# A two-layer graph network: layer 0 with paired logits, moments taken once per step, layer 1's preparation inside step 2, repair by a branch, and masks on ScalarE

## The chip, the cores and the metric

The kernel runs on one core of a Trainium2 chip. The metric is the device time of one execution, in microseconds (us). A core has five engines with queues of their own: PE (TensorE, matrix products; PEld are its weight loads), DVE (VectorE), ACT (ScalarE), POOL (GpSimd) and SP (SyncE, which here issues transfers). Operands lie in SBUF, results of matrix products in PSUM. "Profile" and "trace" below mean one execution recorded by the hardware profiler; its times are from the start of that execution's span.

## The reference, cut to what matters

A graph of N = 3327 nodes with D = 256 features passes through two layers. Each layer normalises its input, applies a relu, runs a graph network and adds the result to its input.

```python
def top_p_attention(X):                       # A: (N, N), rows sum to 1
    q = X @ W1.T @ W2.T                       # 64 wide
    k = X @ W3.T
    probs = softmax(q @ k.T)
    sp = sorted(probs, descending)            # per row
    keep = cumsum(sp) - sp < 0.9
    A = probs * mask(keep)
    return A / A.sum(-1)

# layer 0
h = relu(layernorm(x))
R = adj + I;  R = R / R.sum(-1)
Xf = Xa = h;  Z = 0
for n in range(2):
    A  = top_p_attention(Xa)
    Xf = R @ Xf                               # "full step"
    Xa = A @ Xa                               # "attention step"
    Z  = Z + Xf @ U1[n].T + Xa @ U2[n].T      # "add up"
x = x + layernorm(h + Z) * g + b

# layer 1, 4 heads of 64
h = relu(layernorm(x));  hp = h @ W
s, d = hp . a_src, hp . a_dst                 # per node and head
e = where(adj > 0, leaky_relu(s_i + d_j), -inf)
x = x + elu(softmax(e) @ hp)
```

## The kernel before

The nodes are cut into 26 row tiles of 128 (the last has 127 rows). Everything that is used often stays in SBUF: `main` holds h (with a column of ones, so that a product with it gives row sums as well), `xf1` and `xa1` the two results of step 0. A tile framework puts the instructions of all engines into an order by its own list scheduling, so the order on an engine's queue is not that of the program's text.

**Beginning (L542-557).** All 26 tiles of x are loaded and their moments taken; then one Sqrt for all; then each tile is normalised and passed through a relu.

**Keys (L797-810), once per step.** For each tile: two transposes (L563), the projection by W3 to keys as columns (L571, copied into `kt` at L802), the same as rows (L805), and a product that sums up the keys' second moments and means (L809).

**Pairs of tiles (L811-832).** Row tiles go in 13 pairs. `exponentials` (L574-610) projects the two tiles' queries (L571, L587), multiplies them with the moments (L591), from which DVE gets the mean and variance of each row's logits, and then computes the logits, per tile seven pieces of 512 columns with a depth of 64 (L604), each followed by an exponential on ACT that also sums (L605). The exponentials of the next pair are called before the pair in hand is cut.

**`top_p` (L612-730)** finds for each row the value below which the entries sum to a tenth of the row. A start value comes from the mean and variance by a polynomial, with four ACT calls, Ln and Exp in turn (L630, L631, L633, L645, L648). Then `below` (L655-665) passes over the 3327 entries of each of the two tiles, 3 times in step 0 and 4 times in step 1 (`EVALS`), with some 17 operations on two columns between passes (L672-691). A last pass (L705) writes the entries below a safe bound; from 16 pieces of 208 columns the eight largest are taken (L703), from those the 32 largest (L713, L715), and their running sum tells the cut. L730 zeroes what lies below the cut. How many of the 32 places are used, and some other values, are left in `met`.

**`full_step` (L734-746)** multiplies a tile's column block of the adjacency (two loads of 13 blocks, L739, on SP's queue) with h or xf1: 26 products of 128 rows, each of which the trace records as two instructions (so L741 has 52 per tile), divides by the row sums and writes the next Xf. **`attention_step` (L748-770)** transposes the 26 blocks of a tile's cut exponentials in groups of four (L757, copied at L759) and multiplies them with Xa (L766). In step 1, **`add_up` (L772-793)** loads x once more for h, transposes the four results and multiplies them with U1 and U2.

**Layer 1's preparation (L842-905)** follows when all tiles are done: layernorm, sum with x, a second layernorm and relu, transposes, one product with W and the two attention vectors (L895), and the scaling of hp (L898).

**Layer 1 (L907-999)** takes blocks of four row tiles (the last block two), and for every two column tiles j: a load of adjacency (L939), one mask of up to 1024 columns on POOL (L943), eight products of exponentials with the mask on DVE (L953), eight products with hp into the two halves of two accumulators (L963) and eight of `den` (L968), again two instructions each in the trace. Then each tile is transposed, divided, passed through elu and written (L978-999).

**Verdict (L1004-1034).** From `met` and the reach of s and d comes one flag, `redo`. If it is set, a slower general form computes everything again behind a branch (L1041).

Of the kernel before, what the change touches and what calls it, by code (L numbers as in the profile page):

```python
# [18 lines left out]
P = 128  # L19
N = 3327  # L20
NT = 26
# [20 lines left out]
EVALS = (3, 4)  # L42
AIM = 13.0
WIN = 32
PIECES = 16
PIECE = 208
NC = 7

REACH = 40.0
QUANTILE = (0.0080475, 0.1178442, 0.6505088, 2.0535298, 1.2031906)  # L50
# [416 lines left out]

@with_exitstack
def fast(
    ctx: ExitStack,  # L470
    tc: tile.TileContext,
    redo: bass.AP,
# [15 lines left out]
    V, S, T = nc.vector, nc.scalar, nc.tensor  # L488

    const = ctx.enter_context(tc.tile_pool(name="const", bufs=1))  # L490
    ident = const.tile([P, P], F32, name="ident")
    make_identity(nc, ident)
    eps = const.tile([P, 1], F32, name="eps")
    nc.gpsimd.memset(eps, LN_EPS)
# [3 lines left out]
    mv = const.tile([P, NT, 2], F32, name="mv")  # L498
    rstd = const.tile([P, NT], F32, name="rstd")

    met = const.tile([P, 5, STEPS * NT], F32, name="met")

    def ln_stats(pool, t):
        st = pool.tile([P, V.BN_STATS_DIM], F32, name="bst")
        V.bn_stats(st, main[:, t, :D])
        V.bn_aggr(mv[:, t, :], st)

    def ln_rstd():
        S.activation(rstd, mv[:, :, 1], AF.Sqrt, bias=eps)
        V.reciprocal(rstd, rstd)  # L510

    def ln_apply(dst, src, mean, rs):
        V.tensor_scalar(dst, src, mean, rs, ALU.subtract, ALU.mult)

    with ExitStack() as l0:
        wpool = l0.enter_context(tc.tile_pool(name="wpool", bufs=1))
        w1 = wpool.tile([P, 2, DA], F32, name="w1")
        w3 = wpool.tile([P, 2, DA], F32, name="w3")
        w2 = wpool.tile([DA, DA], F32, name="w2")
        u1 = wpool.tile([P, STEPS, 2, D], F32, name="u1")  # L520
        u2 = wpool.tile([P, STEPS, 2, D], F32, name="u2")
        h_mv = wpool.tile([P, NT, 2], F32, name="h_mv")
        h_rstd = wpool.tile([P, NT], F32, name="h_rstd")
        xf1 = wpool.tile([P, NT, D + 1], F32, name="xf1")
        xa1 = wpool.tile([P, NT, D + 1], F32, name="xa1")
        kt = wpool.tile([DA, NP], F32, name="kt")
        gm = wpool.tile([DA, 2 * DA + 1], F32, name="gm")
        V.tensor_copy(gm[:, :DA], ident[:DA, :DA])

# [3 lines left out]
        apool = l0.enter_context(tc.tile_pool(name="apool", bufs=2))  # L533
        etpool = l0.enter_context(tc.tile_pool(name="etpool", bufs=2))
        fin = l0.enter_context(tc.tile_pool(name="fin", bufs=1))
        ps_l = l0.enter_context(tc.tile_pool(name="ps_l", bufs=2, space=PSUM))
        ps_acc = l0.enter_context(tc.tile_pool(name="ps_acc", bufs=2, space=PSUM))
        ps_t = l0.enter_context(tc.tile_pool(name="ps_t", bufs=2, space=PSUM))
        ps_m = l0.enter_context(tc.tile_pool(name="ps_m", bufs=2, space=PSUM))


        for t in range(NT):  # L542
            nc.sync.dma_start(main[:, t, :D], x[t * P : (t + 1) * P, :])
            ln_stats(small, t)
        nc.scalar.dma_start(w1, w1t.rearrange("(c p) o -> p c o", p=P))
        nc.scalar.dma_start(w3, w3t.rearrange("(c p) o -> p c o", p=P))
        nc.scalar.dma_start(w2, w2t)
        nc.scalar.dma_start(u1, u1t.rearrange("n (c p) o -> p n c o", p=P))
        nc.scalar.dma_start(u2, u2t.rearrange("n (c p) o -> p n c o", p=P))
        ln_rstd()  # L550
        V.tensor_copy(h_mv, mv)
        V.tensor_copy(h_rstd, rstd)
        for t in range(NT):
            ln_apply(main[:, t, :D], main[:, t, :D], mv[:, t, 0:1], rstd[:, t : t + 1])
            S.activation(main[:, t, :D], main[:, t, :D], AF.Relu)
        for z in (main, xf1, xa1):
            nc.gpsimd.memset(z[:, :, D : D + 1], 1.0)

        def transposed(src, t):

            ps = ps_m.tile([P, 2, P], F32, name="pm")
            for c in range(2):
                T.transpose(ps[:, c, :], src[:, t, c * P : (c + 1) * P], ident)  # L563
            xt = small.tile([P, 2, P], F32, name="xt")
            S.copy(xt, ps)
            return xt

        def projected(w, xt):
            ps = ps_m.tile([DA, P], F32, name="pm")
            for c in range(2):  # L570
                T.matmul(ps, w[:, c, :], xt[:, c, :], start=(c == 0), stop=(c == 1))  # L571
            return ps

        def exponentials(src, tiles):  # L574


            G = len(tiles)
            sm = small.tile([P, G], F32, name="sm")
            mu = small.tile([P, G], F32, name="mu")
            sq = small.tile([P, G], F32, name="sq")  # L580
            es = []
            for g, t in enumerate(tiles):
                ps = projected(w1, transposed(src, t))
                ut = small.tile([DA, P], F32, name="ut")
                S.copy(ut, ps)
                ps = ps_m.tile([DA, P], F32, name="pm")
                T.matmul(ps, w2, ut, start=True, stop=True)  # L587
                qt = small.tile([DA, P], F32, name="qt")
                S.copy(qt, ps)
                ps = ps_m.tile([P, 2 * DA + 1], F32, name="pm")  # L590
                T.matmul(ps, qt, gm, start=True, stop=True)  # L591
                qg = small.tile([P, 2 * DA + 1], F32, name="qg")
                S.copy(qg, ps)
                V.tensor_copy(mu[:, g : g + 1], qg[:, 2 * DA :])
                V.scalar_tensor_tensor(
                    qg[:, :DA], qg[:, :DA], 1.0, qg[:, DA : 2 * DA], ALU.mult, ALU.mult, accum_out=sq[:, g : g + 1]
                )
                e = epool.tile([P, NP], F32, name="e")
                nc.gpsimd.memset(e[:, N:], 0.0)  # L599
                parts = small.tile([P, NC], F32, name="parts")  # L600
                for c in range(NC):
                    w = min(512, N - 512 * c)
                    pl = ps_l.tile([P, 512], F32, name="pl")
                    T.matmul(pl[:, :w], qt, kt[:, 512 * c : 512 * c + w], start=True, stop=True)  # L604
                    S.activation(  # L605
                        e[:, 512 * c : 512 * c + w], pl[:, :w], AF.Exp, accum_out=parts[:, c : c + 1]
                    )
                V.tensor_reduce(sm[:, g : g + 1], parts, AX.X, ALU.add)
                es.append(e)
            return es, sm, mu, sq  # L610

        def top_p(es, sm, mu, sq, n, tiles):  # L612
# [4 lines left out]
            G, i0 = len(es), n * NT + tiles[0]  # L617

            def small_tile(name):
                return small.tile([P, G], F32, name=name)  # L620

            b = small_tile("b")
            V.tensor_scalar(b, sm, 1.0 - TOP_P, None, ALU.mult)
            V.tensor_copy(met[:, 0, i0 : i0 + G], sm)
            var = small_tile("var")
            V.tensor_mul(var, mu, mu)
            V.tensor_sub(var, sq, var)
            V.tensor_scalar(var, var, 1e-6, None, ALU.max)
            sg = small_tile("sg")
            S.activation(sg, var, AF.Ln)  # L630
            S.activation(sg, sg, AF.Exp, scale=0.5)  # L631
            u = small_tile("u")
            S.activation(u, b, AF.Ln, scale=1.0 / N)  # L633
            V.tensor_sub(u, u, mu)
            V.scalar_tensor_tensor(u, var, -0.5, u, ALU.mult, ALU.add)
            V.tensor_scalar(u, u, -6.0, -0.3, ALU.max, ALU.min)
            w = small_tile("w")
            V.tensor_scalar(w, u, QUANTILE[0], None, ALU.mult)
            for c in QUANTILE[1:-1]:
                V.scalar_tensor_tensor(w, w, c, u, ALU.add, ALU.mult)  # L640
            V.scalar_tensor_tensor(w, w, QUANTILE[-1], sg, ALU.add, ALU.add)
            t = small_tile("t0")
            V.tensor_mul(t, w, sg)
            V.tensor_add(t, t, mu)
            S.activation(t, t, AF.Exp)  # L645
            g = small_tile("g0")
            V.tensor_mul(g, w, w)
            S.activation(g, g, AF.Exp, scale=0.5)  # L648
            V.scalar_tensor_tensor(g, g, math.sqrt(2 * math.pi) / N, sg, ALU.mult, ALU.mult)
            V.tensor_scalar(g, g, 0.25, None, ALU.min)  # L650

            k2 = small_tile("k2")
            V.scalar_tensor_tensor(k2, t, 225.0, t, ALU.mult, ALU.mult)

            def below(th, outs=None, dst=None):  # L655
                sums = small_tile("sums") if dst is None else dst
                ys = []
                for k, e in enumerate(es):
# [4 lines left out]
                    if outs is not None:  # L663
                        outs(k, y)
# [130 lines left out]
        for n in range(STEPS):  # L795
# [17 lines left out]
            for i, tiles in enumerate(groups):  # L813
                es, sm, mu, sq = ready
                if i + 1 < len(groups):
                    ready = exponentials(srca, groups[i + 1])
# [264 lines left out]
```

## Time and profile before

| | us |
|---|---|
| median of 3 runs (3064.71 to 3064.73) | 3064.73 |
| profiled execution | 3067.3 |
| its span | 3065.5 |
| mean granted PE clock | 0.919 |

| stage of the profiled execution | from, us | to, us |
|---|---|---|
| loads, layernorm and relu | 0 | 24 |
| keys of step 0 | 24 | 110 |
| first exponentials and first cut of step 0 | 110 | 221 |
| pairs of step 0 | 221 | 1129 |
| keys of step 1 | 1129 | 1200 |
| first cut of step 1 | 1200 | 1312 |
| pairs of step 1 | 1312 | 2355 |
| layer 1's preparation | 2355 | 2453 |
| layer 1 | 2453 | 3056 |

Busy time over the whole span: PE 2730.0 (89%), PEld 1727.1, DVE 2379.9 (78%), ACT 832.9 (27%), POOL 384.6 (13%). A share of busy time is a mean over stages with different limits, so the stages are read one by one. In the views below, "x728" is a count, "out<-in" are the program's names and shapes, and "idle before, releaser" is the time in which the engine stood still before a group of instructions, with the instruction that ended most of it. PEclk is the share of full speed that the throttle granted to TensorE. The 26 loads of 128 KB of x took 2.0 to 3.4 us from issue to landing, the adjacency loads of 832 KB 4.5 us.

### The profile page before, as it was taken

The numbers are of one execution on the slowest core, as the hardware profiler recorded it, in microseconds if no ns is written. First come the engines' busy times: TensorE is split into PE (matmuls) and PEld (weight loads), VectorE is DVE, ScalarE is ACT, GpSimd is POOL, SyncE is SP. The second block draws the span as 40 slices with busy tenths as digits, with TensorE's granted clock in tenths as the row PEclk, the third lists the DMA queues.
The fourth block names the chain that finished last, engine by engine and source line by source line (L and its number), as shares of the span: only waits on it lengthen the run. The fifth ranks groups of instructions, "written<-read, shape, count | busy, mean of one in ns | idle before, by whom it ended". The sixth has DMA issues, their size and how long they took to land. (4 is left out here: it accounts for less than half of the span.)

```text
span 3065.5 us, 35025 instructions
## 1 busy us (share of the span) xinstructions
PE 2730.0 (89%) x12508; PEld 1727.1 (56%) x12508; DVE 2379.9 (78%) x5887; ACT 832.9 (27%) x2029; POOL 384.6 (13%) x258
## 2 busy tenths in 40 slices
PE   6949999999999999389999999999996499999997
PEld 4427676666666685157776666666775322222232
DVE  3189888878788820899988888888983798999996
ACT  2423333333333324232333333333221300000000
POOL 0000000000000000000000000000001157656543
PEclk9759899999999999589999999999998799999999
DMA  3001111111111111001111111110111132232221
GB/s 109 23 0 45 45 45 45 45 45 45 45 45 45 45 56 34 0 4 49 49 49 47 48 47 49 37 37 27 49 60 41 32 118 76 72 94 87 85 62 29
DMA packets 77224, 150.87 MB, mean 49 GB/s; under 512 B 5489, under 2 KB 63600, under 8 KB 77040
## 3 DMA queue, kind: packets, MB, share of 16 engines
q1 hardware_dynamic: 74656, 146.56, 15.3%
q8 instruction: 100, 1.64, 0.2%
q10 hardware_dynamic: 2384, 1.98, 0.2%
q14 instruction: 84, 0.69, 0.1%
HBM read 145.11 MB, written 3.41 MB: 48 GB/s over the span
## 5 line engine op out<-in xcount | busy, mean ns | idle before, releaser
L953 DVE SCALAR_TENSOR_TENSOR e<-both,low,mask 128x512 f32<-128x512 f32 (+1 forms) x728 | 518.0, 781 | 21.0 <-POOL mask L943 15.2
L660 DVE SCALAR_TENSOR_TENSOR y<-e,nt 128x3327 f32<-128x3327 f32 x130 | 478.8, 3683 | 2.3
L604 PE MATMUL pl<-kt,qt 64*128 64x512 f32 (+1 forms) x728 | 408.8, 701 | 53.4 <-ACT e L605 53.4
L759 ACT COPY et<-pt 128x512 f32<-128x512 f32 (+1 forms) x364 | 199.4, 555 | 739.1 <-PE pt L757 739.1
L963 PE MATMUL acc<-e,hp 128*64 128x512 f32 (+1 forms) x1456 | 366.0, 578 | 3.2 <-DVE e L953 3.1
L943 POOL TENSOR_SCALAR mask<-adjb 128x1024 bf16<-128x1024 f32 (+1 forms) x91 | 322.0, 3546 | 240.1 <-DVE e L953 168.3
L741 PE MATMUL acc<-main,at 128*128 128x257 f32 x1352 | 335.1, 400 | 0.8 <-DMA at<-in_adjt_dram 0.8
L741 PE MATMUL acc<-xf,at 128*128 128x257 f32 x1352 | 334.1, 396 | 0.3 <-ACT xa L770 0.3
L766 PE MATMUL acc<-xa,et 128*128 128x257 f32 x1352 | 322.5, 382 | 3.8 <-ACT et L759 3.8
L766 PE MATMUL acc<-main,et 128*128 128x257 f32 x1352 | 323.2, 382 | 0.2
L604 PEld LDWEIGHTS pl<-kt,qt 64*128 64x128 f32 x728 | 144.8, 223 | 291.7 <-ACT e L605 228.4
L741 PEld LDWEIGHTS acc<-main,at 128*128 128x128 f32 x1352 | 261.2, 199 | 52.6 <-issue 13.3
L757 PE MATMUL pt<-ident,e 128*128 128x128 f32 x1352 | 202.1, 274 | 94.0 <-DVE e L730 94.0
L741 PEld LDWEIGHTS acc<-xf,at 128*128 128x128 f32 x1352 | 255.3, 197 | 48.8 <-issue 14.0
L766 PEld LDWEIGHTS acc<-xa,et 128*128 128x128 f32 x1352 | 245.2, 191 | 36.8 <-ACT et L759 7.6
L766 PEld LDWEIGHTS acc<-main,et 128*128 128x128 f32 x1352 | 244.9, 190 | 35.5 <-ACT et L759 6.2
L599 POOL MEMSET e<- 128x1 f32 x52 | 4.9, 98 | 2013.5 <-PE pt L757 1090.1
L605 ACT ACTIVATE e<-pl 128x512 f32<-128x512 f32 (+1 forms) x364 | 205.1, 564 | 154.4 <-PE pl L604 151.4
L757 PEld LDWEIGHTS pt<-ident,e 128*128 128x128 f32 x1352 | 168.6, 141 | 127.7 <-DVE e L730 95.2
L703 DVE MAX8 cands<-y 128x8 f32<-128x208 f32 x832 | 237.2, 360 | 0.5
L963 PEld LDWEIGHTS acc<-e,hp 128*64 128x64 f32 x1456 | 104.1, 136 | 226.3 <-DVE e L953 125.5
L968 PE MATMUL den<-e,qd 128*32 128x512 f32 (+1 forms) x1456 | 200.9, 582 | 0.0
(186 smaller groups left out, 2656.3 us busy)
## 6 DMA issues: line engine op xcount, KB each, us to landing
at<-in_adjt_dram SPq DMA_DIRECT2D x104, 832.0 KB, 4.5
adjb<-in_adjt_dram SPq DMA_DIRECT2D x78, 512.0 KB, 3.8
main<-in_x_dram SPq DMA_DIRECT2D x26, 128.0 KB, 3.4
xh<-in_x_dram SPq DMA_DIRECT2D x26, 128.0 KB, 2.0
xr<-in_x_dram SPq DMA_DIRECT2D x26, 128.0 KB, 2.1
adjb<-in_adjt_dram SPq DMA_DIRECT2D x13, 256.0 KB, 2.8
out_dram<-r SPq DMA_DIRECT2D x25, 128.0 KB, 1.7
u<-in_u1t_dram ACTq DMA_DIRECT2D x1, 512.0 KB, 5.8
```

What stands on the lines that cost most here:

```text
L604: T.matmul(pl[:, :w], qt, kt[:, 512 * c : 512 * c + w], start=True, stop=True)
L605: S.activation(e[:, 512 * c : 512 * c + w], pl[:, :w], AF.Exp, accum_out=parts[:, c : c + 1])
L660: V.scalar_tensor_tensor(y, e[:, :N], th[:, k : k + 1], e[:, :N], ALU.is_lt, ALU.mult, accum_out=sums[:, k : k + 1])
L703: V.max(cands[:, k, c, :], y[:, c * PIECE : min(c * PIECE + PIECE, N)])
L741: T.matmul(acc, at[:, j - j0, :], src[:, j, :], start=(j == 0), stop=(j == NT - 1))
L757: T.transpose(pt[:, k, :], e[:, (j0 + k) * P : (j0 + k + 1) * P], ident)
L759: S.copy(et[:, :n, :], pt[:, :n, :])
L766: T.matmul(acc, et[:, j - j0, :], src[:, j, :], start=(j == 0), stop=(j == NT - 1))
L943: nc.gpsimd.tensor_scalar(mask[:, :, :n, :], adjb[:, :n].rearrange("p i j q -> p j i q"), 0.0, None, ALU.is_gt)
L953: V.scalar_tensor_tensor(e[:, k, :w], both[:, k, :w], low[:, j, k : k + 1], mask[:, j - j0].rearrange("p i q -> p (i q)")[:, :w], ALU.max, ...
L963: T.matmul(acc[k // 2][half, :w], hp[:, j, k, :], e[:, k, :w], start=(j == 0), stop=(j == NT - 1))
L968: T.matmul(den[32 * k : 32 * k + 32, :w], qd[:, j, k : k + 1].to_broadcast([P, 32]), e[:, k, :w], start=(j == 0), stop=(j == NT - 1), tile ...
```

## The change

The numbers of lines are those of the changed kernel from here on.

**Beginning.** Each tile is normalised on its own: moments on DVE, the inverse root as a power on GpSimd (`normal`, L507-516), normalisation and relu as one ACT call.

**Keys and queries together (L614-665).** W1 and W2 are multiplied once into one matrix, and `wqk` holds it beside W3, so that one product (L626) gives a tile's queries in one half of the 128 rows and its keys in the other; even and odd tiles have the halves in turn. The keys are also copied to the other half by a transfer from SBUF to SBUF (L629), on SP's queue. So `kt` holds all keys twice, and `qq` the queries of an even tile in rows 0 to 63 and those of the odd one in rows 64 to 127. Mean and variance of the logits of all rows are computed once per step, behind the keys (L649-665), instead of per pair.

```diff
-                    T.matmul(pl[:, :w], qt, kt[:, 512 * c : 512 * c + w], start=True, stop=True)
+                for g in range(2):
+                    half = slice(g * DA, g * DA + DA)
+                    T.matmul(pl[:, g, :w], qq[half, i, :], kt[half, lo : lo + w], start=True, stop=True)
```

**`top_p` (L685-812).** The start value is worked out on GpSimd, with a power in place of the logarithms, and two Exp forms on ACT:

```diff
-EVALS = (3, 4)
+EVALS = (2, 4)
...
-            S.activation(sg, var, AF.Ln)
-            S.activation(sg, sg, AF.Exp, scale=0.5)
...
-            S.activation(u, b, AF.Ln, scale=1.0 / N)
...
+            GP.tensor_mul(v, b, cn[:, both])
+            GP.tensor_scalar(v, v, math.exp(-6.0), math.exp(-0.3), ALU.max, ALU.min)
+            GP.tensor_tensor(v, v, powers[:, 2, :2], ALU.pow)
+            GP.tensor_scalar(w, v, QUANTILE[0], QUANTILE[1], ALU.mult, ALU.add)
+            GP.tensor_mul(w, w, v)
+            GP.tensor_scalar(w, w, QUANTILE[2], None, ALU.add)
+            GP.tensor_mul(w, w, v)
+            GP.tensor_add(w, w, zadd[:, both])
```

Step 0 has one pass of `below` fewer. The passes write what nobody reads as BF16. The last pass (L776) goes over each tile in two halves, and the eight largest are taken from 13 pieces of 256. The final mask (L808) also sums what it keeps, so that the attention step needs no column of ones.

**`full_step` (L816-836)** loads pieces of 7 blocks into three buffers (before, 13 into two), and has an accumulator of its own beside that of the attention. The row sums are kept from step 0 for step 1. The transposes, the projections and `add_up` share one PSUM pool of two buffers, `ps_x`. In the program's text the attention of a pair now stands ahead of its full steps.

**`add_up` (L861-907)** takes in all of layer 1's preparation: x is loaded, the two layernorms and the sum are done for one tile, the new x is written to DRAM (`x1s`, L888, SP's queue), the transposes and the product with W follow at once (L895, L900), and `main` takes hp in place of h. The weights of layer 1 are prepared at the beginning (`layer1_weights`, L595).

**Repair.** After each step, `amend` (L964-993) works out a flag for each row tile and one over all, and branches on it; behind the branch stands, for each tile, another branch around `search_again` (L909-962), which computes the tile's logits again, finds the cut bit by bit and repeats the tile's attention (in step 1 its full step and `add_up` too):

```diff
+            with tc.If(nc.values_load(flags[:, NT:], min_val=0, max_val=1) > 0):
+                for t in range(NT):
+                    with tc.If(nc.values_load(flags[:, t : t + 1], min_val=0, max_val=1) > 0):
+                        search_again(n, t)
...
+            for bit in range(BITS - 1, -1, -1):
+                V.tensor_scalar(cand.bitcast(I32), cut.bitcast(I32), 1 << bit, None, ALU.bitwise_or)
+                y = scr.tile([P, N], BF16, name="y")
+                V.scalar_tensor_tensor(y, e[:, :N], cand, e[:, :N], ALU.is_ge, ALU.mult, accum_out=sums)
+                V.tensor_tensor(ok, sums, th, ALU.is_ge)
+                V.copy_predicated(cut, ok, cand)
```

The flag at the end, `again`, depends on the reach of s and d alone, and the general form stands behind it as before.

**Layer 1 (L1023-1120).** The masks move to ACT, in two passes, and x is read back from DRAM at the end of a tile:

```diff
+                S.activation(adjb[:, :n], adjb[:, :n], AF.Relu)
                 mask = mpool.tile([P, JC, K, P], BF16, name="mask")
-                nc.gpsimd.tensor_scalar(
-                    mask[:, :, :n, :], adjb[:, :n].rearrange("p i j q -> p j i q"), 0.0, None, ALU.is_gt
-                )
+                S.activation(mask[:, :, :n, :], adjb[:, :n].rearrange("p i j q -> p j i q"), AF.Sign)
...
+                x1 = opool.tile([P, D], F32, name="x1", bufs=4)
+                nc.sync.dma_start(x1, x1s[t])
```

## The prediction

> **What bounds the kernel now.** First the busy time by stretches: the keys of step 0, its start, one pair of row tiles in step 0 and one in step 1, layer 1's preparation, one block of four tiles in layer 1.
>
> ```profile
> core 0: us, PE busy (x) PEld busy (x) DVE busy (x) ACT busy (x) POOL busy (x), PEclk, DMA share, GB/s
> 24.00:110.00 86.00, 77.66 (x430) 53.24 (x430) 10.22 (x35) 33.03 (x112) 2.55 (x26) 1.00 0.12 41
> 110.00:222.00 112.00, 65.92 (x124) 28.41 (x124) 67.39 (x205) 39.64 (x102) 0.00 (x0) 0.50 0.00 0
> 578.00:656.00 78.00, 74.69 (x319) 54.48 (x318) 61.31 (x168) 26.37 (x63) 0.20 (x2) 0.93 0.16 50
> ...
> 1730.00:1818.00 88.00, 83.13 (x370) 61.82 (x369) 75.43 (x198) 29.06 (x67) 0.20 (x2) 0.96 0.15 48
> 2355.00:2455.00 100.00, 38.76 (x174) 29.13 (x175) 72.02 (x220) 26.05 (x85) 25.25 (x28) 0.69 0.16 49
> 2650.00:2740.00 90.00, 86.92 (x445) 24.39 (x443) 84.81 (x123) 5.40 (x10) 59.93 (x17) 0.98 0.28 81
> ```
>
> PE (second figure) fills the pairs, DVE is close behind; at the start and in the preparation neither is full. Layer 1 has PE and DVE both near full. Then the groups, for who waits for whom:
>
> ```profile
> L953 DVE SCALAR_TENSOR_TENSOR e<-both,low,mask 128x512 f32<-128x512 f32 (+1 forms) x728 | 518.0, 781 | 21.0 <-POOL mask L943 15.2
> L660 DVE SCALAR_TENSOR_TENSOR y<-e,nt 128x3327 f32<-128x3327 f32 x130 | 478.8, 3683 | 2.3
> L604 PE MATMUL pl<-kt,qt 64*128 64x512 f32 (+1 forms) x728 | 408.8, 701 | 53.4 <-ACT e L605 53.4
> ...
> L757 PE MATMUL pt<-ident,e 128*128 128x128 f32 x1352 | 202.1, 274 | 94.0 <-DVE e L730 94.0
> ```
>
> The last figure of L757 is the start of each step: PE idle 94.0 in two waits for the first mask. L604's 53.4 is PE waiting for the exponentials. Last the timeline of one layer 1 block:
>
> ```profile
> 2619.37 21.09 DVE L953 SCALAR_TENSOR_TENSOR e<-both,low,mask 128x512 f32<-128x512 f32 x27
> ...
> 2626.34 3.15 POOL L943 TENSOR_SCALAR mask<-adjb 128x1024 bf16<-128x1024 f32 x1 [2.94 <-DVE e L953]
> ...
> 2632.43 3.14 POOL L943 TENSOR_SCALAR mask<-adjb 128x1024 bf16<-128x1024 f32 x1 [2.94 <-DVE e L953]
> ```
>
> One mask, so eight e (two j, four heads), every 6.09 us. An e lasts 740 ns at least, and one beside each mask 1520. So the stages end at 110 (keys 0), 221 (first attention), 1129 (step 0), about 1200 and 1312 (the same in step 1), 2355, 2453 and 3056; the span is 3065.5, the profiled time 3067.3. The median shown, 3064.7, is 2.6 less, which I take off at the end.
>
> **The change, part by part.**
>
> **Start to first attention, 221 to 170.** The barrier over all 26 moments goes, so PE starts near 8 instead of 24. Keys take 26 x 1.5 (eight small matmuls at .15 to .3) = 39; 3.7 full steps that the emitted order puts among them 46 (52 matmuls at .237 = 12.35 per tile); seven paired logits 6.4: end at 100. Each tile's keys also go to the other 64 rows by a DMA on SP's queue, between the adjacency loads (nearest rows: x's 128 KB, 2.0 to 3.4 us); the next tile's work covers it, and without that cover it would cost up to 3.4 once, at the last tile. New moments: four matmuls, products and 52 narrow matmuls, 8; their chain of nine small operations at .195 with one exponential 3. GpSimd's start value follows: ten links, between .1 (its 128x1 memset, 98 ns) and .84 (its 128x256 neg) each, no small arithmetic being in this trace; I take .3, nearer the memset in size: 3, ends 1 to 8.4. It replaces four ACT calls whose table loads alone took 4 x 1.28. ACT's exponential of the start value (L711) waits for this chain, and behind it in ACT's queue stand copies of transposes (L850) for which PE waits. top_p of step 0: four passes at 3.61 (L660 start to start) 14.4; two rounds of small operations 27 x .195 = 5.3, and a few before and behind 1; window 7.3; 26 MAX8 at .33 (.276 for 208, scaled) 8.6; two tiles' wins 5.2; two masks 7.2: 49. In DVE's emitted order two passes of the next pair stand ahead of the mask: 7.2. Sum 8 + 39 + 46 + 6.4 + 11 + 3 + 49 + 7.2 = 169.6. Gain 51.
>
> **Step 0, 908 to 772.** Rows 0-63 and 64-127 work side by side in the paired logits. L604 takes .454 per 512 columns; in L963, whose column halves lie side by side already, one takes .224 to .264, about half. So a pair's logits go from 12.7 + 2.4 stall to 6.4, and are then held by 14 exponentials at .60 on ACT: 8.4. One query and three small projections per tile go from inside the pairs to the keys. A pair then is full steps 24.7 + attention 29.5 (as timed in one pair) + 8.4 + 1.4 fill = 64 on PE, while DVE needs 49 + 5 = 54 (one secant pass per tile fewer). Six full steps (74) are emitted before the first attention and owed no longer, so the first four pairs run at DVE's 54. 4 x 54 + 7 x 64 + 54 + 53.5 for the end = 772. If the halves didn't run side by side, a pair is 70.
>
> **The branch after a step, 10 each.** Twelve small DVE operations 2.3, a matmul, and loads of a flag into every engine that branches; the end of the kernel shows one such load and branch as 3065.5 - 3056.4 = 9.1 together with its shutdown. Ends 4 and 20. Nothing hides it: all queues stand at it.
>
> **Keys of step 1 to first attention, 182 as 80 + 11 + 3 + 70 + 7 = 171.** 80 as in step 0, less x; top_p has two more rounds (2 x (7.2 + 3.3)).
>
> **Step 1, 1043 to 1097.** DVE: 28.9 for passes, 7.3 window, 8.6, 5.2, 7.2, 14 of small operations, and layer 1's preparation, which comes in here: two tiles x 3 (moments .41 + .17 twice, and four 128x256 operations at .42): 77. PE: 24.7 + 29.5 + 8.4 + two add-ups at 5.5 + 2 x 1.4 (L890 and L895) = 76.5. Before: 88 by PE 83 and DVE 75. But the loop is not free: logits of pair i+2 wait for buffers of pair i, then the start value, two passes, the mask of pair i+1, its attention and add-up, which share two PSUM buffers (ps_x) with the transposes. Against a floor of 78 and 10 for each link that DVE's order puts in front (two passes 7.2, start value 3), I take 86; ends 78 and 96. 12 x 86 + 65 for the last = 1097. The x1 rows written to DRAM stand on SP's queue ahead of adjacency loads (832 KB, 4.5 us to land); three buffers of 7 blocks instead of two of 13 cover 21 matmuls, 5.0 us, so a write that waits for DVE longer than that shows up as a PE wait for at.
>
> **Preparation, 98 to 8.** It leaves only layer 1's broadcasts and first mask. Its cover is the pair above; if DVE binds there, its 6 per pair return.
>
> **Layer 1, 603 to 539.** Masks go to ACT: two passes of 1024 at .832 ns per element (512 and 256 copies .585, .372) = 2.1 per pair of j, in an engine busy 5.4 of 90. Then DVE is 8 x .665 = 5.33, and PE 3.58 + 1.85 = 5.43 (acc with DVE ahead, den): 5.45 instead of 6.08. 91 x .63 = 57; less the 7 of its own start, 539. Masks on ACT may bring table loads at 1.28 beside 8 exponentials per block: 20 of 71, hidden. x1 read back: 26 loads of 128 KB, 2.0 each, hidden behind den.
>
> The Trainium skill's page "ScalarE: Activation LUTs" (Rules for kernel authors) wants relu and the like on VectorE. By the row of a 256-wide DVE TENSOR_SCALAR, .305 start to start, a 1024 mask is at most 1.2 there, which makes DVE 5.33 + 1.2 = 6.5 per pair of j, more than now; ACT is the better place here.
>
> **Sum.** 170 + 772 + 10 + 171 + 1097 + 10 + 8 + 539 + 9 = 2786; less 2.6, 2783.
>
> **The rivals.**
>
> *GpSimd is blocked by DVE's passes.* For: the e beside each POOL mask doubled, 740 to 1520 ns, so the two engines do stop each other. Against: that mask is 1024 wide, the new operations two. If each of ten links waits half a pass, 1.8, the chain is 21 instead of 3. In the pairs of both steps half of that is outside the cover of DVE's other work: 24 x 6 + 2 x 18 = 180. 2963; with a third of it 2845.
>
> The Trainium skill's page "SBUF — State Buffer" (Who interferes with whom) says a DVE instruction with two SBUF inputs contends with a GpSimd instruction that reads SBUF, the other then blocking for the whole of it. It speaks against this start value; taken at a full pass per link it makes the chain 36 and the time some 3100. The trace shows the doubling for e alone.
>
> *The halves of the paired logits run one after the other.* L963's row speaks against. 26 x 4.3 less what DVE hides in step 1: 2783 + 90 = 2873.
>
> *The loop of step 1 is covered, and PE binds at 78 a pair.* 12 x 8 = 96 less, 10 in step 0: 2677. For: DVE had 61 of 78 busy with the same passes while PE ran free.
>
> *Slower: repair is taken.* A tile whose search fails costs 27 passes at 3.61 + .8 = 119, eight more passes 29, logits, copies and exponentials 12, attention 15: 175, and nothing overlaps it, since it stands in a branch. The gain is 282; two failing tiles and it is gone: 3133. One row of 3327 is enough for a tile. For: step 0 has one secant pass fewer and a cheaper start value. Against: before, too, a failing row sent the kernel through the general form, and its time shows none; the search, worked through in single precision on the reference's inputs, leaves 1 to 23 of its 32 places used, so some rows are near the lower end.
>
> **How the numbers follow.** My sum .60, own range 2720 to 2850; blocked GpSimd .15; halves in turn .07; covered loop .10; repair or anything slower .06 (.01 of it near no change); two or three small losses together fill the last .02, at 2850 to 2930. The time is that of the first, 2783. Ends that matter: 12 x 8 or 10 in step 1, 57 in layer 1 if nothing is won there, 2 x 10 at the branches. 2660 leaves out about .04 below, 2940 about .14 above (most of the first rival, and the last). What a measurement here can tell from no change is 0.2%, some 6 us. Faster .93, same .01, slower .06.
>
> **What would show it.** The first attention near 170; one pair in steady step 0 at 64 with ACT, not PE, behind the logits; step 1 at 86 with PE waiting for the mask of L808; no DVE stretch of e above 750 ns and 5.45 per pair of j; each branch some 10 of empty queues. A chain of GpSimd operations longer than 5, with gaps the length of a pass, is the first rival; instructions of search_again in the trace (27 passes in a row) are the last. It is wrong above all if step 1's pairs lie outside 78 to 96, since that counts twelvefold.

## The result, and the profile after

The changed kernel takes 3278.2 us in the median of 4 runs (3272.5 to 3281.7) against 3064.7 before: the ratio is 1.069, interval 1.067 to 1.071. The forecast was 2783. It is the last rival that came: two row tiles of step 1 go through the repair.

This is the changed kernel by stretches of the profiled execution (span 3279.8 us): keys of step 0, its first cut, one pair of step 0, one of step 1, the repair, one block of layer 1. The columns are those of the first table in the prediction.

```profile
core 0: us, PE busy (x) PEld busy (x) DVE busy (x) ACT busy (x) POOL busy (x), PEclk, DMA share, GB/s
24.00:134.00 110.00, 96.59 (x490) 62.19 (x488) 29.00 (x156) 36.63 (x101) 18.57 (x64) 0.92 0.23 66
134.00:218.00 84.00, 67.42 (x243) 44.84 (x241) 56.82 (x144) 13.05 (x47) 20.38 (x30) 0.79 0.20 58
600.00:666.00 66.00, 59.98 (x288) 46.77 (x287) 48.81 (x122) 17.96 (x49) 6.64 (x16) 0.99 0.19 56
1820.00:1901.00 81.00, 72.94 (x350) 57.76 (x346) 73.65 (x184) 21.97 (x56) 15.16 (x26) 0.96 0.17 49
2225.00:2697.00 472.00, 100.65 (x348) 70.32 (x348) 294.80 (x331) 28.75 (x47) 5.23 (x12) 0.57 0.04 11
2790.00:2873.00 83.00, 82.33 (x432) 22.12 (x426) 71.75 (x117) 31.66 (x39) 4.76 (x4) 1.00 0.33 95
```

A pair of step 0 went from 78 to 66, one of step 1 from 88 to 81, a block of layer 1 from about 89 to 83. The fifth line is new: 472 us in which PE is busy for a fifth. The groups of the page say what runs there:

```profile
L848 PE MATMUL px<-ident,e 128*128 128x128 f32 x1404 | 218.2, 282 | 359.8 <-DVE e L948 269.9
...
L936 DVE SCALAR_TENSOR_TENSOR y<-e,cand 128x3327 bf16<-128x3327 f32 x54 | 199.0, 3686 | 1.8
```

L936 is a pass of the bitwise search in `search_again`, 27 to a tile; x54 are two tiles. L848, the transposes of the repaired tile's exponentials, idles 269.9 for L948, the last operation of that search that writes them, in two waits. The count of L848 says the same: 1404 = 54 x 26, where 52 tiles and steps need 1352.

### The profile page after: what moved, and what is told of

Same layout as the page of the kernel before. It is cut to its first block, busy times and chain, and to the rows that moved or that the text cites. A ratio compares the mean times of both kernels' runs of the same rounds, so it can differ in the third digit from the quotient of the medians.

```text
span 3279.8 us, 35848 instructions
## 1 busy us (share of the span) xinstructions
PE 2580.6 (79%) x12414; PEld 1697.5 (52%) x12414; DVE 2420.4 (74%) x5386; ACT 818.1 (25%) x1853; POOL 377.9 (12%) x706
## 3 DMA queue, kind: packets, MB, share of 16 engines
q10 hardware_dynamic: 2656, 2.05, 0.2%
## 5 line engine op out<-in xcount | busy, mean ns | idle before, releaser
L848 PE MATMUL px<-ident,e 128*128 128x128 f32 x1404 | 218.2, 282 | 359.8 <-DVE e L948 269.9
L850 ACT COPY et<-px 128x512 f32<-128x512 f32 (+1 forms) x378 | 204.5, 556 | 822.6 <-PE px L848 822.2
L848 PEld LDWEIGHTS px<-ident,e 128*128 128x128 f32 x1404 | 180.1, 146 | 404.2 <-issue 288.0
L729 DVE SCALAR_TENSOR_TENSOR y<-e,nt 128x3327 bf16<-128x3327 f32 x104 | 383.0, 3683 | 1.8
L826 PE MATMUL accf<-xf,at 128*128 128x256 f32 x1456 | 363.4, 396 | 5.3 <-DVE xf L835 5.2
L857 PE MATMUL acca<-main,et 128*128 128x256 f32 x1352 | 334.3, 393 | 40.4 <-ACT et L850 40.3
L857 PE MATMUL acca<-xa,et 128*128 128x256 f32 x1456 | 356.5, 391 | 10.7 <-ACT et L850 10.7
L826 PE MATMUL accf<-main,at 128*128 128x257 f32 x1352 | 330.9, 396 | 23.7 <-issue 18.9
L1078 PE MATMUL acc<-e,main 128*64 128x512 f32 (+1 forms) x1456 | 347.3, 577 | 0.7 <-DVE e L1068 0.7
L826 PEld LDWEIGHTS accf<-xf,at 128*128 128x128 f32 x1456 | 278.7, 199 | 59.9 <-issue 11.9
L826 PEld LDWEIGHTS accf<-main,at 128*128 128x128 f32 x1352 | 259.5, 198 | 74.4 <-issue 29.5
L857 PEld LDWEIGHTS acca<-xa,et 128*128 128x128 f32 x1456 | 271.7, 196 | 49.3 <-ACT et L850 17.6
L680 PE MATMUL pl<-kt,qq 64*128 64x512 f32 (+1 forms) x728 | 253.8, 652 | 26.6 <-ACT e L682 25.5
L776 DVE SCALAR_TENSOR_TENSOR y<-e,up 128x1536 f32<-128x1536 f32 x104 | 202.7, 1949 | 2.9
L936 DVE SCALAR_TENSOR_TENSOR y<-e,cand 128x3327 bf16<-128x3327 f32 x54 | 199.0, 3686 | 1.8
```

What stands on the lines that cost most here:

```text
L680: T.matmul(pl[:, g, :w], qq[half, i, :], kt[half, lo : lo + w], start=True, stop=True)
L729: V.scalar_tensor_tensor(y, e[:, :N], th[:, k : k + 1], e[:, :N], ALU.is_lt, ALU.mult, accum_out=sums[:, k : k + 1])
L776: V.scalar_tensor_tensor(y[:, : hi - lo], e[:, lo:hi], up[:, k : k + 1], e[:, lo:hi], ALU.is_lt, ALU.mult, accum_out=halves[:, k, a : a + 1],)
L826: T.matmul(acc[:, :w], at[:, j - j0, :], src[:, j, :w], start=(j == 0), stop=(j == NT - 1))
L848: T.transpose(pt[:, k, :], e[:, (j0 + k) * P : (j0 + k + 1) * P], ident)
L850: S.copy(et[:, :m, :], pt[:, :m, :])
```

## The experiments

All kernels are compared with the kernel before on their own chip, where that took 3078 to 3092 us. Where only one execution was timed, the time stands without an interval.

**Which check set the flag.** Sixty branches behind step 1 read it out; each has one marker on DVE as its body:

```diff
+            V.tensor_tensor(conds[:, 2], met[:, 1], met[:, 3], ALU.is_gt)
+            V.tensor_tensor(conds[:, 3], met[:, 2], met[:, 4], ALU.not_equal)
...
+            for k in range(2 * K):
+                with tc.If(nc.values_load(flags2[:, k : k + 1], min_val=0, max_val=1) > 0):
+                    V.memset(mark, 0.0)
```

> The changed kernel, with sixty small branches behind step 1 that read out, for row tiles 4 and 20 (the two that the trace shows being repaired), which of the five conditions set the flag, the number of the row, and how many of the 32 window places it used. Theory A (the coarser pieces, 13 of 256 for 16 of 208, lose a ninth candidate): the third condition, the eighth largest of a piece above the cut, is set in both, with 8 to 28 places used and one row per tile. Rival B (the new start value sends a row's search astray): the first or second condition, 32 or 0 places used. Rival C (ties or rounding in the halved last pass): the fourth. Time some 60 x 2 us over the changed kernel's 3278, so 3400.

It took 3318 us, 40 more than the changed kernel, where 120 more was expected. In its trace the marker's row is the answer, and below it two of the markers one by one:

```profile
L1039 DVE MEMSET mark<- x24: 59/59/59, 2705.8 to 2741.2; 128x1 f32 x24
...
2720.40 0.06 DVE L1039 MEMSET mark<- 128x1 f32 x1 [0.62 <-DVE mark L1039]
2726.55 0.06 DVE L1039 MEMSET mark<- 128x1 f32 x1 [6.09 <-DVEq L1038]
```

24 of the 60 branches were taken. Their starts fit a step of about 0.68 us from branch to branch (between the two shown lie nine steps, 6.15), which gives each marker its place in the order: in both tiles only the fourth condition is set, `met[2] != met[4]`; each has one row; 12 to 15 of the 32 places are used; the rows are 33 of tile 4 and 17 of tile 20, rows 545 and 2577 of the graph. Theory A and rival B fall, and rival C is left. The fourth condition is true when the value kept last and the one dropped first are the same number: a tie at the cut.

Worked out in double precision from the reference's inputs, the two logits at the cut of row 545 differ by 1.1e-6, those of row 2577 by 1.6e-6. Of the 3327 rows of step 1 both are among the dozen smallest gaps; the median is 5.1e-4. One rounding step of a logit near 1.2 is 1.2e-7, and each logit is a sum of 64 rounded products, so such pairs can come out equal. What the marker shows to be equal are the exponentials; whether the logits on the chip were equal too, no run reads out.

**What the change is worth without the repair.** The flags are multiplied by zero; the branch stays, the repair is left out:

```diff
+            V.tensor_scalar(bad, bad, 0.0, None, ALU.mult)
             ps = ps_x.tile([1, NT], F32, name="px")
             T.matmul(ps, ones, bad, start=True, stop=True)
```

> The changed kernel with the flags multiplied by zero, so that the branch after each step stays and no tile is repaired; it leaves the repair out. By the trace of the changed kernel the repair of step 1 lasts from 2225 to 2697, 472 us, and layer 1 then starts with a slow clock. Theory (the rest of the change gains what the sum said): 3278 - 472 = 2806, or down to 2790 if layer 1 also gains its start. Rival (the change loses elsewhere too, the repair being only part): above 3000.

2810.6 us, ratio 0.909 (0.908 to 0.911), and no pass of L936 in the trace. The theory holds, at 5 us above the end of its range: the repair is all that made the kernel slower. The kernel before took 3088.6 on this chip, 24 more than where the forecast was made, and the forecast of 2783 was a ratio of 0.908.

**Finer pieces.**

```diff
-PIECES = 13
-PIECE = 256
+PIECES = 16
+PIECE = 208
```

> The changed kernel with 16 pieces of 208, as before the change, in place of 13 of 256, everything else as it is. Theory A (the pieces are too coarse): no repair in the trace, time as with the flag held at zero plus 6 more MAX8 per pair at .12 more each in all: 2800 to 2820. Rival B (start value) or C: the same two repairs, 3278 within 15. Something between, one repair: about 3040.

3270.3 us, ratio 1.059 (1.057 to 1.061), again 54 passes of L936. Theory A falls here too; the pieces have no part in it, as the probe said.

**Masks of layer 1 on POOL again** (with the flags at zero):

```diff
-                S.activation(adjb[:, :n], adjb[:, :n], AF.Relu)
                 mask = mpool.tile([P, JC, K, P], BF16, name="mask")
-                S.activation(mask[:, :, :n, :], adjb[:, :n].rearrange("p i j q -> p j i q"), AF.Sign)
+                nc.gpsimd.tensor_scalar(
+                    mask[:, :, :n, :], adjb[:, :n].rearrange("p i j q -> p j i q"), 0.0, None, ALU.is_gt
+                )
```

> The flags held at zero as in the second run (it leaves the repair out), and the masks of layer 1 on POOL again as before the change. Theory (each POOL mask stretches one e from .74 to 1.5 us, and a pair of j takes 6.08 instead of 5.45 or so): 57 above the second run, 45 to 60. Rival (PE binds at its own pace either way, so the engine of the mask is no matter): within 15 of the second run.

2864.7 us, ratio 0.928 (0.926 to 0.929): 54 more than the run with the flags at zero on the same chip, where 45 to 60 was expected, so the rival falls. The products with the mask in layer 1, in the trace of this run and then in that with the flags at zero (the line has moved by one):

```profile
L1070 DVE SCALAR_TENSOR_TENSOR e<-both,low,mask 128x512 f32<-128x512 f32 (+1 forms) x728 | 510.7, 772 | 45.0 <-POOL mask L1060 40.0
```
```profile
L1069 DVE SCALAR_TENSOR_TENSOR e<-both,low,mask 128x512 f32<-128x512 f32 (+1 forms) x728 | 465.7, 710 | 41.4 <-issue 24.8
```

The stretched ones are gone with POOL's masks: the longest goes from 1527 to 902 ns, the mean from 772 to 710, which over 728 of them is 45 of the 54 us.

**Ties tolerated.** A tie now counts only if what it drops weighs more than a thousandth of the row. Where it doesn't, the mask drops all entries equal to the cut, so that an entry which the reference keeps is left out.

```diff
-            V.tensor_tensor(one, met[:, 2], met[:, 4], ALU.not_equal)
+            V.tensor_sub(one, met[:, 2], met[:, 4])
+            V.tensor_mul(one, one, met[:, 3])
+            V.scalar_tensor_tensor(one, met[:, 0], 1e-3, one, ALU.mult, ALU.is_lt)
```

> The changed kernel, where two equal values at the cut set the flag only if the values dropped weigh more than a thousandth of the row; the other four conditions, the branch and the repair stay. Theory (only the tie condition was set, and each tie weighs one entry of some 2100 kept): no repair, time of the run with the flags held at zero plus two small operations in each step: 2806 to 2816. Rival (another condition is near its bound, or a tie that weighs more): one repair or two, 3020 to 3280.

2802.4 us, ratio 0.908 (0.905 to 0.912), no repair: 4 below the range expected, but on another chip than the run with the flags at zero. By the double-precision row sums an entry at the cut of row 545 weighs 3.43 of 23217, 1.5e-4. This version beats both kernels, and it still repairs what the other four conditions find.

**Another rounding, nothing else.** If the ties are luck, scaling one product by the smallest step must change which rows tie:

```diff
-            S.copy(w1r, ps)
+            S.activation(w1r, ps, AF.Copy, scale=1.0 + 2.0**-23)
```

> The changed kernel with the product of W1 and W2 scaled by 1 + 2^-23 on the way, so that every logit is rounded anew and nothing else differs. Theory (ties of rounding: among 3327 rows of step 1 the cut gaps have a median of 5e-4 in the logit, so that a gap of about one rounding step, 1.2e-7, is met by about 0.5 rows in a draw): rows 545 and 2577 are free with high odds, and the number of tiles repaired is drawn again: none .6 (2810), one .3 (about 3085), more .1. Rival (something systematic in these two tiles, a half of rows or a place in the search): tiles 4 and 20 again, 3278.

2805.1 us, no repair. A second draw, with 1.0 - 2.0**-22:

> As the first draw, with 1 - 2^-22: another rounding of all logits of the changed kernel. Theory (about 0.5 ties in a draw): again rows of its own or none: none .6 (2805), one .3 (3083, the price of one forced tile), two .1 (3280). Rival (tiles 4 and 20 are special and the first draw missed them by accident): tile 4 or 20 again.

2802.5 us, no repair. Tiles 4 and 20 aren't special; three roundings of the same kernel gave 2, 0 and 0 tiles.

The same two draws on the kernel before, at its projection by W1 (L585):

```diff
-                S.copy(ut, ps)
+                S.activation(ut, ps, AF.Copy, scale=1.0 + 2.0**-23)
```

> The kernel before, with the projection by W1 scaled by 1 + 2^-23, so that its logits are rounded anew. Its flag has the same tie condition, and a tie sends it through the general form behind the branch. Theory (the kernel before owes its time to a draw without a tie): no tie with .6, then 3065 to 3090 as before; a tie with .4, then the general form is added, which computes everything again without the search, far above 4000. Rival (its search can't tie): 3065 to 3090 in every draw.

> The kernel before with 1 - 2^-22 in the same place. As for the run ahead of it: .6 as before, .4 far above 4000; both draws without a tie have .36 by the theory, so that they would not settle it.

3089.8 and 3086.3 us beside 3091.8: no tie in either. As expected ahead of the runs, that settles nothing on how often the kernel before meets one.

**The price of one tile.** Flags at zero, but that of tile 4 set in step 1:

```diff
             V.tensor_scalar(bad, bad, 0.0, None, ALU.mult)
+            if n == 1:
+                V.tensor_copy(bad[:, 4:5], ident[:, :1])
```

> The run with the flags held at zero, but the flag of row tile 4 set in step 1, so that one tile is repaired whatever the search says. It separates the price of a tile from that of the chain of 26 branches. Theory, from the trace of the changed kernel (195 to 204 a tile, 26 branches of 2.75 = 72, some 8 around them): 2810 + 200 + 72 + 8 = 3090. Rival (price all in the tile, 472 / 2): 3046.

3082.5 us: 272 more than with the flags at zero (2810.6, on another chip), 280 more than the version that tolerates ties (2802.4, on this chip), and the time of the kernel before on this chip, 3082.0. That is near the 3090 of the theory, and the rival's 3046 falls. Two stretches of its trace: the bitwise search, and the branches behind the repaired tile.

```profile
2260.00:2380.00 120.00, 3.91 (x19) 3.10 (x17) 115.30 (x136) 0.51 (x1) 0.00 (x0) 0.53 0.00 0
...
2430.00:2520.00 90.00, 8.36 (x25) 4.33 (x26) 4.72 (x10) 8.28 (x12) 0.00 (x0) 0.50 0.14 41
```

In the second, nothing runs for most of 60 us: the engines go through 21 flags that are not set. So one tile gives 195 and the walk over the flags, with what lies around it, some 75 to 85; a second tile in the same walk adds about 200 (3278 - 3082 = 196).

**The price of a tie in the kernel before.** Its flag is held at one, so the general form computes all a second time:

```diff
-        V.tensor_scalar(redo, bad[:1, :1], 1.0, None, ALU.min)
+        V.tensor_scalar(redo, bad[:1, :1], 0.0, 1.0, ALU.mult, ALU.add)
```

> The kernel before with its flag held at one, so that the general form behind the branch runs after the fast one, as it would after one tie; it gives the price of a tie in the kernel before. Theory (the general form finds every tile's cut bit by bit, 27 passes at 3.61 for 52 tiles and steps, beside the same attention, full steps and layer 1): 52 x 27 x 3.61 = 5070, plus some 1000 to 2500 of other work: 3080 + 6000 to 7600 = 9100 to 10700. Rival (a cheap general form): below 7000.

11831.8 us, more than the 9100 to 10700 expected. The passes cost what was expected (1404 of them, 5124 us busy in its trace), so what was sized too small is the other work, some 3600 us instead of 1000 to 2500. So the repair bounds an event that would nearly quadruple the time of the kernel before.

**The weights' product first.** The block that multiplies W1 and W2 is moved ahead of the loop over the tiles of x (on the version that tolerates ties):

```diff
+        w1 = etpool.tile([P, 8, DA], F32, name="et")
...
         for t in range(NT):
             xt = main[:, t, :D]
...
-        w1 = etpool.tile([P, 8, DA], F32, name="et")
```

> The fifth run's kernel (ties tolerated), with the product of W1 and W2 ahead of the loop over the 26 tiles of x in the program's text. In the trace with the flags at zero PE waited 17.6 us for the copies of W1 (L587), which stand behind the tiles' relu calls in ACT's queue, and began the keys at 23 instead of 8. Theory (this wait is the head of the chain to the first attention): 10 to 15 less than the fifth run. Rival (the keys are bound by what arrives, x and its moments, or by PE's own work up to the first cut): within 4.

2797.2 us, ratio 0.907 (0.904 to 0.910), 5 less, with intervals that overlap; in the traces the first attention is at 212.9 instead of 219.5. Neither number expected came. PE's wait for the copies of W1 is this row (total, count, longest), of the version ahead and then of the moved one:

```profile
PE px L589 <- ACT w1r L587: 17.3, 2, 11.2
```
```profile
PE px L578 <- ACT w1r L576: 11.6, 2, 11.3
```

One wait of 11 is left in both; the copy of W1 still runs behind the first relu of x on ACT, since the program's text does not set the order of the queue. Only the second wait, about 6, went.

## Why the prediction was wrong, and where it was right

**The step that failed** is in the last rival, "the search, worked through in single precision on the reference's inputs, leaves 1 to 23 of its 32 places used, so some rows are near the lower end", and the .06 that followed from it. The sum had no term for the repair, which took 472 us. The rival asked whether the window is wide enough. The condition that struck is the tie, and a working in another order of rounding can't say whether the chip's sums tie: that is a draw, whose chance was to be had from the gaps. That the time before showed no general form was one such draw too. 3327 rows, a density of gaps of 0.69 / 5.1e-4 = 1350 per unit of logit near zero (from the median), times one rounding step of 1.2e-7: 0.54 rows in step 1, so a chance of about .4 for at least one. That is an estimate, by the logits alone; the three draws of the changed kernel (2, 0, 0) are in keeping with it. With .4 on the repair the range had to hold 3080.

**The price of that rival** was too small as well: 175 a tile, 3133 with two. The traces give 195 and 204. Passes 118 (119 in the sum), but the logits and the first maximum with empty queues and PE at half clock (0.57 from 2225 to 2260) 24 instead of 12, and add-up and layer 1's preparation of the tile, 14, had been left out. And 26 branches inside the branch were left out altogether: about 73 in the changed kernel's trace (472 less the two tiles).

**The rest of the sum**, against the run with the flags at zero:

| term | predicted | measured |
|---|---|---|
| start to first attention | 170 | 224 |
| step 0, to the branch behind it | 772 | 776 |
| branch, keys of step 1, first cut | 181 | 190 |
| step 1 | 1097 | 1039 |
| branch and start of layer 1 | 18 | 14 |
| layer 1 | 539 | 558 |
| end | 9 | 9 |
| sum | 2786 | 2810 |

Some 0.8% of each measured figure can be the chip's, as said above (3088.6 against 3064.7 for the kernel before). By the ratio the sum is right to a thousandth, and that is luck: its largest misses, 54 more at the start and 58 less in step 1, cancel. The 54 are made up of three things. PE began the keys at 23, not 8, because of the wait for W1's copies. The keys then took 112 us to the first product of the moments, where 39 + 46 + 6.4 was taken; 3.5 full steps lay among them, as forecast. And from there to DVE's first pass it was 32 instead of 14. The cut itself took 54, where 56 was taken. In both steps the products of the moments alone last 22 to 23 us, costed at 8. This is the timeline of the run with the flags at zero in step 1, and then its table by stretches:

```profile
1083.35 1.12 PE L649 MATMUL acca<-qq,gbd 128*128 128x512 f32 x2
...
1094.47 2.05 PE L649 MATMUL acca<-qq,gbd 128*128 128x512 f32 x2
...
1106.60 4.49 POOL L660 TENSOR_TENSOR sig<-stat,powers 128x26 f32<-128x26 f32 x1 [20.12 <-DVE stat L659]
```
```profile
1080.00:1086.00 6.00, 6.00 (x25) 2.86 (x24) 1.20 (x3) 1.65 (x10) 0.00 (x0) 1.00 0.02 5
...
1092.00:1100.00 8.00, 8.00 (x25) 4.99 (x24) 0.69 (x1) 1.26 (x4) 0.00 (x0) 0.50 0.01 2
```

The same product takes 1.12 and then 2.05: the granted clock goes from 1.00 to 0.50 between them, although PE's records fill both stretches, the second mostly with products of two columns. And one power over 26 columns, costed as one small operation of .2, takes 4.5 with DVE waiting.

*Pairs.* Step 0 at 66 (64 predicted). Step 1 at 81 to 83 (86): the loop is covered better than I took it, between my forecast and the rival with 78. *Layer 1.* The 57 for the masks is shown by the undone part, 54; the stage missed by 19, though not in the steady e: in the middle of a block a pair of j takes 5.44 (5.45 forecast), 13 of them 71 of a block's 81 to 83, so the rest lies around the ends of the blocks. One e lasts 902 ns and 146 others up to 759, where 750 was named as a sign of being wrong. *Branches.* One that is not taken costs about 5 of the 10 at layer 1 and next to nothing behind step 0, where PE goes on with full steps of step 0 up to it (59.2 of 60 us busy from 940 to 1000) and waits 0.5 there.

*Halves of the logits.* They are no bound: 26 of the 28 records of a pair's logits took 8.2 (617.7 to 625.9), with waits for ACT's exponentials, as 8.4 had it; one half after the other would be 12.7.

*GpSimd blocked.* This rival came in part, and it has a price. In 17 of the 26 pairs the start value's nine operations took 3.0 to 3.8, about as predicted, since DVE waits for them. In seven, one or two of them fell beside a pass or a mask of DVE and were stopped, and the chain took 6.4 to 9.8; the first pair of each step waits for the moments. And one operation behind the chain falls beside a pass in most pairs (the timeline of the run with the flags at zero, one pair of step 0):

```profile
627.34 0.22 POOL L699 TENSOR_SCALAR b<-met 128x2 f32<-128x2 f32 x1 [34.77 <-DVE met L697]
...
628.23 0.71 POOL L704 TENSOR_TENSOR v<-v,powers 128x2 f32<-128x2 f32 x1
...
630.17 0.19 POOL L709 TENSOR_TENSOR w<-w,zadd 128x2 f32<-128x2 f32 x1
630.82 3.69 DVE L729 SCALAR_TENSOR_TENSOR y<-e,t 128x3327 bf16<-128x3327 f32 x1 [3.07 <-ACT t L711]
631.21 3.35 POOL L718 TENSOR_TENSOR w<-w 128x2 f32<-128x2 f32 x1 [0.84 <-ACT t L711]
...
634.59 0.20 ACT L719 ACTIVATE g<-w 128x2 f32<-128x2 f32 x1 [3.52 <-POOL w L718]
634.70 1.05 ACT L850 COPY et<-px 128x512 f32<-128x512 f32 x2
...
635.32 3.78 PE L857 MATMUL acca<-main,et 128*128 128x256 f32 x8 [3.14 <-ACT et L850]
635.50 0.17 DVE L748 TENSOR_SCALAR x<-g 128x2 f32<-128x2 f32 x1 [0.99 <-POOL g L721]
```

L718 multiplies two columns; L709, of the same form, takes 0.19. L718 starts when the first pass of DVE has, ends when that pass ends, and lasts about 3.35 in 20 of the 26 pairs. What waits for it is the slope g: its first use on DVE (L748) stands between the two passes and waits 0.99. Its exponential (L719) stands in ACT's queue ahead of the copies of transposes (L850), and PE waits 3.1 us for those in each of seven pairs of step 0, and 7.3 and 8.0 in two where the chain was stopped as well: 42 us of waits for L850 over step 0. They stand in the measured 776; what would be won without them no run shows. The prediction named this place in ACT's queue, for L711. For L718 the trace agrees with the Trainium skill's page "SBUF — State Buffer", section Who interferes with whom: a DVE instruction with two SBUF inputs and a GpSimd instruction that reads SBUF shut each other out for the whole instruction.

*Slips in the working.* In this rival's price, half of the chain's 18 is 9 a pair and not 6, which makes it 3035 and not 2963, and a third of its 180 is 2843. Three buffers of 7 blocks cover 21 products, which are 42 records at .237, 10 us and not 5.0. The row of the 256-wide DVE operation on x has .32 from start to start, not .305. None of these changed the forecast.

## What to carry to other kernels

A branch that is hardly ever taken is priced by the chance that the data take it, and that chance comes from the data, not from one trial: for a check on equal numbers it is the number of rows, times a rounding step, over the usual gap. A condition that sends work to a slow path should ask whether the event matters to the result, not whether it happened. And a path behind a branch starts with empty queues and a slow PE: count each of its stages in full, and the walk over flags that are not set. Last, a small operation on one engine can hold up a third: look at what stands behind its reader in the queue.

## What the runs showed of the hardware

A chain of 26 branches on loaded values, hardly any taken, costs about 2.8 us for each flag, with all engines standing (0.00 PE, ACT and POOL busy):

```profile
2431.00:2476.00 45.00, 0.00 (x0) 0.00 (x0) 0.63 (x3) 0.00 (x0) 0.00 (x0) 0.50 0.05 11
```

That is the changed kernel between its two repaired tiles, 16 flags. It is not the price of any branch: the probe's 60, each around one instruction on DVE, lay 0.68 apart. Whether the length of the body or the number of engines makes the difference, no run here tells. GpSimd's power took 0.71 us for two columns and 4.5 for 26, where its product of two columns took 0.19.
